# A weighted sum of gathered rows: kept in PSUM, with one pair of rows added ahead of the transposes

## The chip, the cores and the metric

One Trainium2 chip (trn2), one of its cores. The metric is the device time of one run in microseconds (us). The engines are called PE (TensorE; PEld is its weight load), DVE (VectorE), ACT (ScalarE), POOL (GpSimd, which also issues the indirect gathers) and SP (SyncE).

## The reference

Two graph layers over 3327 nodes with 512 features; the adjacency matrix `adj` is sparse (about 0.24% of it is set) and has a full diagonal. After each layer the input is added and the row is normalised. Layer 0 is a graph attention with 4 heads. Layer 1, which the change concerns, is cut here to its core:

```python
type_sum = adj @ x                                   # plain sum of the neighbours' rows
attn_a = sigmoid(concat([type_sum, x]) @ Wa.T + ba)  # one gate per node; attn_b likewise
h = x @ W_sa
scores = (h @ a_left)[:, None] + (h @ a_right)[None, :]
e = where(adj != 0, exp(-leaky_relu(scores, 0.01)), 0)
x_a = (e / (sum(e, axis=1) + 1e-5)) @ h              # weighted sum of the neighbours
x_b = adj @ (x @ W_gcnb) + b_gcnb                    # plain sum, projected
x = layernorm(x + sigmoid(attn_a * x_a + attn_b * x_b))
```

Since the projections are linear, a node needs two sums over its neighbours' rows of `x`: a weighted one (projected with `W_sa`) and a plain one (projected with `W_gcnb`).

## The kernel before, in words

Nodes are padded to 3328 and sorted by degree within two groups, so that 26 tiles of 128 nodes have few neighbour slots each: `CAPS` lists 4 to 14 per tile, 226 in all. Layer 0 leaves a table of rows in HBM (`table1`: 512 features and 8 columns of scores). For a tile, POOL issues one indirect gather per slot (`indirect`, L615), which brings one neighbour row for each of the 128 nodes into a slot of a ring of 42 row buffers in SBUF (`ring`). The node's own row is in SBUF already (`row1`). Two tiles (`T0`) have a further row, the "stair", for the few nodes with more neighbours; that makes 228 gathers in layer 1.

The tiles go through a software pipeline written out by hand: a loop over `i` in which tile `j` is summed, the next tile `j1` gets its weights, `jp` (the previous one) is projected, and `jpp` (the one before that) is gated, added and normalised. Within each engine instructions run in the order in which the loop writes them. One turn of the loop, by engine:

- POOL: `gather` issues every gather whose slots belong to a tile that was freed (`free(jp)`), then, when all gathers are out, the results are scattered to `out` (L146).
- PE: `turn(jp)` transposes the weighted sum (L1107), `plain_sum(j)` builds the plain sum, already transposed, by transposing the tile's own row and every neighbour row into one PSUM tile where they accumulate (L1098, four 128x128 transposes a row), and `project(jp, 1)`, `project(jp, 0)` multiply both sums of the previous tile by their weights (L1118, 16 matmul instructions).
- DVE: `weighted(j, 0)` runs the first part of the weighted sum, one multiply-add per slot (L1085: `sw = row * e + sw`, 128x512 fp32, all operands in SBUF), then come the gating of `jpp` (L1147, L1148, with the projections in PSUM as second input), the scores and weights of `j1` (`weights_a`, L1032 to L1052), the rest of the sum (`weighted(j, 1)`), the addition for `jpp` (L1171), `weights_b(j1)` (L1059 to L1062) and the statistics of `jpp` (L692, L693 and, for every fourth tile or so, the chain L701 to L708).
- ACT: copies of the two transposed sums to SBUF (`to_sbuf`, L1112), tanh and exp, and `scaled_first(j1)` (L1070), which starts the next weighted sum with the own row times its weight.

Each L1085 needs the result of the one before it. The cut between the two parts of a tile's sum:

```python
cut = 2 + (CAPS[j] * 5 + 7) // 8
for s0, n, g, _ in got[j]:
    for i in range(n):
        s = s0 + i
        if (s < cut) == (part == 0):
            nc.vector.scalar_tensor_tensor(sw, g[:, i, 0:F], e[:, s : s + 1], sw, ALU.mult, ALU.add)
```

[...]

Of the kernel before, what the change touches and what calls it, by code (L numbers as in the profile page):

```python
# [8 lines left out]
F32 = mybir.dt.float32  # L9
AF = mybir.ActivationFunctionType  # L10
ALU = mybir.AluOpType
# [3 lines left out]
P = 128  # L15
# [10 lines left out]
CAPS = (14, 12, 11, 10, 9, 9, 8, 8, 7, 6, 6, 5) + (14, 13, 11, 10, 10, 9, 9, 8, 8, 7, 7, 6, 5, 4)  # L26
# [52 lines left out]
def sparse_pass(  # L79
# [39 lines left out]
    nc = tc.nc  # L119
    N, F = out.shape  # L120
    NP = x.shape[0]
    H, FO = a_self.shape
    KT = F // P
# [5 lines left out]
    T0 = (0, NG[0])  # L129
    B = len(STAIRS)  # L130
# [45 lines left out]
    def place(j):  # L176

        return (0, j) if j < NG[0] else (1, j - NG[0])
# [5 lines left out]
    def row1(j):  # L184
        g, i = place(j)
        return x1[g][:, i, :]

    def slots(j):

        return S + 1 if j in T0 else CAPS[j] + 1  # L190
# [419 lines left out]
    got, stair = {}, {}  # L610
# [44 lines left out]
    def gather():  # L655

        while waiting and waiting[0][0] - freed[0] <= RING:
            indirect(*waiting.pop(0)[1:])

    def free(j):  # L660

        freed[0] = ends_at[j]
# [285 lines left out]
    for i in range(NT + 3):  # L948
# [10 lines left out]
        if 0 < i <= NT:  # L959
            j = order0[i - 1]  # L960
# [7 lines left out]
            if done:  # L968
                k0, scale, shift = done
# [30 lines left out]
    m1 = ctx.enter_context(tc.tile_pool(name="m1", bufs=2))  # L1000
    ps1 = ctx.enter_context(tc.tile_pool(name="ps1", bufs=1, space=PSUM, side="right"))
# [12 lines left out]
        order += long[:1] + short[:1]  # L1014
        short, long = short[1:], long[1:]
    order += last
    ew, gates, sums, plain, proj, zs, stair_sum = {}, {}, {}, {}, {}, {}, {}

    def own_score(j):
        ew[j] = m1.tile([P, S + 1], F32, tag="e", name=f"e{j}", bufs=3)  # L1020
        nc.scalar.copy(ew[j][:, 0:1], row1(j)[:, F + 6 : F + 7])

    def weights_a(j):

        c = slots(j)
        e = ew[j]
        gate = gates[j] = m1.tile([P, 12], F32, tag="gate", name=f"gate{j}", bufs=5)
        if j in T0:
            small = ps1.tile([P, B * H], F32, tag="small", name=f"to_nodes1_{j}")
            cols = to_nodes(m1, small, f"l1_{j}", stair[j][:, F : F + 3])  # L1030
        for s0, n, g, _ in got[j]:
            nc.vector.tensor_scalar(e[:, s0 : s0 + n], g[:, :n, F], row1(j)[:, F + 3 : F + 4], None, ALU.add)  # L1032
        if j in T0:
            nc.vector.scalar_tensor_tensor(
                e[:, C0 + 1 :], cols[:, :, 0], row1(j)[:, F + 3 : F + 4], no_step, ALU.add, ALU.subtract
            )
        nc.vector.scalar_tensor_tensor(e[:, :c], e[:, :c], 0.01, e[:, :c], ALU.mult, ALU.max)

        nc.scalar.activation(e[:, :c], e[:, :c], AF.Exp, scale=-1.0, accum_out=gate[:, 2:3])
        for i, (s0, n, g, _) in enumerate(got[j]):  # L1040
            nc.vector.tensor_reduce(
                gate[:, 4 + 2 * i : 6 + 2 * i], g[:, :n, F + 1 : F + 3].rearrange("p s i -> p i s"), AX.X, ALU.add
            )
        parts = len(got[j])
        if j in T0:
            nc.vector.tensor_reduce(
                gate[:, 4 + 2 * parts : 6 + 2 * parts], cols[:, :, 1:3].rearrange("p b i -> p i b"), AX.X, ALU.add
            )
            parts += 1
        nc.vector.tensor_add(gate[:, 0:2], gate[:, 4:6], row1(j)[:, F + 4 : F + 6])  # L1050
        for i in range(1, parts):
            nc.vector.tensor_add(gate[:, 0:2], gate[:, 0:2], gate[:, 4 + 2 * i : 6 + 2 * i])  # L1052

        nc.scalar.activation(gate[:, 0:2], gate[:, 0:2], AF.Tanh, scale=0.5)

    def weights_b(j):

        c, e, gate = slots(j), ew[j], gates[j]
        nc.vector.tensor_scalar(gate[:, 2:3], gate[:, 2:3], 1e-5, None, ALU.add)  # L1059
        nc.vector.tensor_scalar(gate[:, 0:2], gate[:, 0:2], 0.5, 0.5, ALU.mult, ALU.add)  # L1060
        nc.vector.reciprocal(gate[:, 2:3], gate[:, 2:3])
        nc.vector.tensor_scalar(e[:, :c], e[:, :c], gate[:, 2:3], gate[:, 0:1], ALU.mult, ALU.mult)  # L1062
        if j in T0:
            small = ps1.tile([P, B * H], F32, tag="small", name=f"to_rows1_{j}")
            ws2[j] = to_rows(m1, small, f"l1_{j}", e[:, C0 + 1 :].rearrange("p (b o) -> p b o", o=1))

    def scaled_first(j):

        sw = sums[j] = m1.tile([P, F], F32, tag="sw", name=f"sw{j}")
        nc.scalar.activation(sw, row1(j)[:, 0:F], AF.Copy, scale=ew[j][:, 0:1])  # L1070
        if j in T0:
            scaled = m1.tile([P, F], F32, tag="scaled", name=f"scaled{j}", bufs=1)
            nc.scalar.activation(scaled, stair[j][:, 0:F], AF.Copy, scale=ws2[j])
            stair_sum[j] = ps1.tile([P, F], F32, tag="stair", name=f"stair_sum{j}")
            nc.tensor.matmul(stair_sum[j], to_node, scaled, start=True, stop=True)  # L1075

    def weighted(j, part):

        e, sw = ew[j], sums[j]
        cut = 2 + (CAPS[j] * 5 + 7) // 8  # L1080
        for s0, n, g, _ in got[j]:
            for i in range(n):
                s = s0 + i
                if (s < cut) == (part == 0):
                    nc.vector.scalar_tensor_tensor(sw, g[:, i, 0:F], e[:, s : s + 1], sw, ALU.mult, ALU.add)  # L1085
        if part == 1 and j in T0:
            nc.vector.tensor_add(sw, stair_sum[j], sw)

    def plain_sum(j):


        pl = plain[j] = ps.tile([P, KT, P], F32, tag="acc", name=f"acc1_{j}", bufs=2)
        rows = [row1(j)] + [g[:, i, :] for _, n, g, _ in got[j] for i in range(n)]
        rows += [stair[j]] if j in T0 else []
        for i, row in enumerate(rows):
            steps = j in T0 and i == len(rows) - 1
            for k in range(KT):
                nc.tensor.matmul(  # L1098
                    pl[:, k, :], row[:, k * P : (k + 1) * P], to_node if steps else ident,
                    start=(i + k == 0), stop=(i == len(rows) - 1 and k == KT - 1), is_transpose=not steps,  # L1100
                )

    def turn(j):
# [10 lines left out]
    def project(j, half):  # L1114
        sT, wt = zs[j, half], (wsa, wg)[half]
        po = proj[j, half] = ps1.tile([P, F], F32, tag=f"po{half}", name=f"po{half}_{j}", bufs=1 + half)
        for k in range(KT):
            nc.tensor.matmul(po, sT[:, k, :], wt[:, k, :], start=(k == 0), stop=(k == KT - 1))  # L1118
# [12 lines left out]
    for i in range(NT + 3):  # L1131
        j, j1, jp, jpp = at_(i), at_(i + 1), at_(i - 1), at_(i - 2)
        if i > 0 and jp is not None:
            free(jp)
        gather()
        if j1 is not None:
            own_score(j1)
        if jp is not None:
            to_sbuf(jp, 1)
            turn(jp)  # L1140
            to_sbuf(jp, 0)
        if j is not None:
            plain_sum(j)
            weighted(j, 0)
        if jpp is not None:
            za = zs[jpp] = m1.tile([P, F], F32, tag="za", name=f"za{jpp}", bufs=3)
            nc.vector.tensor_add(za, bias_g, proj[jpp, 1])  # L1147
            nc.vector.scalar_tensor_tensor(za, za, gates[jpp][:, 1:2], proj[jpp, 0], ALU.mult, ALU.add)  # L1148
            nc.scalar.activation(za, za, AF.Tanh, scale=0.5)  # L1149
        if jp is not None:  # L1150
            project(jp, 1)
            project(jp, 0)
        if j1 is not None:
            weights_a(j1)
        if j is not None:
            weighted(j, 1)
        if ready:
            k0, scale, shift = ready
            for k in range(k0, i - 2):
                z = row1(order[k])[:, 0:F]  # L1160
                nc.scalar.activation(
                    z, z, AF.Identity, scale=scale[:, k - k0 : k - k0 + 1], bias=shift[:, k - k0 : k - k0 + 1]
                )
                outs.append((own(order[k]), z))
            ready = None
        while outs and not waiting:
            scatter("out", out, *outs.pop(0), N - 1)
        if jpp is not None:
            za = zs[jpp]
            zs[jpp] = row1(jpp)[:, 0:F]  # L1170
            nc.vector.scalar_tensor_tensor(zs[jpp], za, 0.5, zs[jpp], ALU.mult, ALU.add)  # L1171
        if j1 is not None:
            weights_b(j1)
            scaled_first(j1)
        if jpp is not None:
            ready = norm.add(i - 2, zs[jpp])
# [452 lines left out]
```

## Time and profile before

| | |
|---|---|
| median of 3 runs | 899.11 us (894.95 to 904.59) |
| profiled execution: its time, its span | 897.77 us, 895.8 us |
| first gather of layer 1 starts | 530.9 us |
| last gather of layer 1 ends | 843.4 us |
| layer 1's multiply-adds (L1085) | 226, first at 542.4 us, last ends at 865.5 us |
| last transpose of a weighted sum (L1107) starts | 872.3 us |
| granted PE clock over the span | 0.908 |

The profile is one execution seen by the hardware profiler. A line of the groups gives the kernel's line, the engine, the operation, output<-inputs, shape and count, then busy time and mean duration, then the engine's idle time ahead of these instructions and what ended it. A line of the timeline gives start, duration, engine, line, operation and, in brackets, the idle time before and its releaser. In both, an engine that waits for nothing is not necessarily the bound: it may stand ready while the data of another are late.

### The profile page before, as it was taken

To read this page: it belongs to the slowest core of one execution; us is meant where nothing else is said; L and a number is where in the kernel's file an instruction comes from. 1 tells how busy PE (TensorE), PEld (TensorE's weight loads), DVE (VectorE), ACT (ScalarE), POOL (GpSimd) and SP (SyncE) were. 2 spreads that over 40 slices of the span, in tenths; PEclk is the share of its full clock that TensorE was granted. 3 is DMA by queue.
4 is the path that set the end of the run, shared out by engine and by line. 5 is a ranking of instruction groups with operands and counts; after the bars stand their busy time and mean duration, and the time that the engine had idled before them with its cause. 6 is when DMAs were issued, how large, how long until landed. Compare 5 with 4: busy or idle time off the path is not lost. (4 is left out here: it accounts for less than half of the span.)

```text
span 895.8 us, 11378 instructions
## 1 busy us (share of the span) xinstructions
PE 745.3 (83%) x3118; PEld 457.4 (51%) x3118; DVE 693.3 (77%) x2032; ACT 272.0 (30%) x794; POOL 595.2 (66%) x641
## 2 busy tenths in 40 slices
PE   4698997416799978799999957987997999999992
PEld 3477775103445534344444435654764666666551
DVE  4288787896678858769898845957996999998973
ACT  0122221002335525444646512212222222232231
POOL 6711133566577777777777747777777777777772
PEclk9799999556899989889999967999898999999997
DMA  8989999999777878789777637677767777777641
GB/s 330 369 340 403 366 377 345 380 387 399 267 225 227 276 234 263 231 278 329 219 234 228 222 115 203 188 199 201 187 184 196 192 196 195 203 193 199 195 187 74
DMA packets 73352, 224.74 MB, mean 251 GB/s; under 512 B 12736, under 2 KB 16784, under 8 KB 72384
## 3 DMA queue, kind: packets, MB, share of 16 engines
q0 software_dynamic: 46368, 153.69, 56.9%
q1 hardware_dynamic: 24256, 68.13, 19.9%
q10 hardware_dynamic: 2656, 2.10, 0.7%
q8 instruction: 27, 0.44, 0.2%
q14 instruction: 45, 0.37, 0.1%
HBM read 203.02 MB, written 31.51 MB: 262 GB/s over the span
## 5 line engine op out<-in xcount | busy, mean ns | idle before, releaser
L615 POOL DMA_INDIRECT ring<-table,srt x464 | 475.7, 1025 | 162.1 <-issue 56.2
L803 PE MATMUL acc<-ring,ident 128*128 128x512 f32 x504 | 239.4, 619 | 18.9 <-DVE ring L802 12.9
L1085 DVE SCALAR_TENSOR_TENSOR sw<-ring,e,sw 128x512 f32<-128x512 f32 x226 | 169.8, 751 | 10.7 <-ACT sw L1070 4.2
L803 PEld LDWEIGHTS acc<-ring,ident 128*128 128x128 f32 x504 | 94.4, 196 | 130.3 <-issue 74.3
L371 PE MATMUL pf<-w,xc 128*128 128x260 f32 x416 | 102.9, 410 | 13.1 <-DVE w L311 13.1
L1098 PE MATMUL acc<-ident,ring 128*128 128x128 f32 x904 | 108.6, 280 | 6.2 <-DMA ring<-table,srt 6.1
L797 DVE TENSOR_TENSOR ring<-ring,w 128x512 f32<-128x512 f32 x176 | 111.8, 693 | 0.5
L1098 PEld LDWEIGHTS acc<-ident,ring 128*128 128x128 f32 x904 | 103.6, 145 | 8.1 <-DMA ring<-table,srt 8.1
L1118 PE MATMUL po<-wsa,sT 128*128 128x512 f32 x208 | 95.4, 602 | 4.6 <-DVE za L1148 2.3
L371 PEld LDWEIGHTS pf<-w,xc 128*128 128x128 f32 x416 | 84.1, 205 | 29.3 <-DVE w L311 13.8
L1118 PE MATMUL po<-wg,sT 128*128 128x512 f32 x208 | 93.6, 593 | 0.0
L795 ACT ACTIVATE ring<-ring,w 128x128 f32<-128x128 f32 x304 | 91.5, 390 | 0.0
L383 POOL DMA_DIRECT2D table<-row x26 | 14.2, 549 | 85.2 <-ACT st L380 82.6
L1118 PEld LDWEIGHTS po<-wsa,sT 128*128 128x128 f32 x208 | 39.7, 193 | 56.6 <-issue 56.1
L1118 PEld LDWEIGHTS po<-wg,sT 128*128 128x128 f32 x208 | 37.5, 190 | 37.3 <-issue 37.3
L1149 ACT ACTIVATE za<-za 128x512 f32<-128x512 f32 x26 | 16.4, 630 | 127.7 <-DVE za L1148 127.7
L402 PE MATMUL pc<-at,pow 128*32 128x512 bf16 (+1 forms) x182 | 23.3, 413 | 35.3 <-DMA at<-in_adjB 25.4
L762 ACT ACTIVATE w<-w 128x40 f32<-128x40 f32 (+10 forms) x26 | 6.2, 237 | 127.5 <-DVE w L761 127.5
L375 ACT COPY row<-pf 128x512 f32<-128x512 f32 x26 | 15.2, 586 | 95.4 <-PE pf L371 49.7
L834 PEld LDWEIGHTS pcol<-v,xt 128*128 128x128 f32 x208 | 28.7, 201 | 14.5 <-issue 12.1
L828 ACT COPY xt<-x1t 128x512 f32<-128x512 f32 x26 | 15.2, 584 | 62.9 <-PE x1t L822 62.9
L402 PEld LDWEIGHTS <-pow 128*32 128x32 bf16 x182 | 7.3, 97 | 47.9 <-issue 44.8
(252 smaller groups left out, 918.4 us busy)
## 6 DMA issues: line engine op xcount, KB each, us to landing
at<-in_adjB SPq DMA_DIRECT2D x78, 512.0 KB, 11.5
ring<-table,srt POOLq DMA_INDIRECT x464, 3.9
table<-row POOLq DMA_DIRECT2D x26, 260.0 KB, 6.1
xc<-in_xB SPq DMA_DIRECT2D x6, 1024.0 KB, 8.4
own<-in_xo SPq DMA_DIRECT2D x1, 3640.0 KB, 46.5
own<-table SPq DMA_DIRECT2D x1, 3640.0 KB, 55.2
at<-in_adjL SPq DMA_DIRECT2D x13, 256.0 KB, 9.9
table<-in_xo SPq DMA_DIRECT2D x1, 3120.0 KB, 27.2
```

The source lines that it names most:

```text
L371: nc.tensor.matmul(pf[:, hh, :HC], xc[:, k, o : o + P], w0[:, k, hh, :], start=(k == 0), stop=(k == KT - 1))
L375: nc.scalar.copy(row[:, 0:F].rearrange("p (h o) -> p h o", h=2), pf[:, :, 0 : F // 2])
L402: nc.tensor.matmul(pc[32 * c : 32 * c + 32, : nt * P], pow2[:, s, :], loaded[i, m], start=(s == 0), stop=(m + 1 not in ms or s == 3),)
L615: return nc.gpsimd.indirect_dma_start(out=out_, out_offset=None, in_=table, in_offset=bass.IndirectOffsetOnAxis(ap=ap, axis=0)).ins
L795: nc.scalar.activation(gv[:, h, :], gv[:, h, :], AF.Copy, scale=w[:, s, h : h + 1])
L797: nc.vector.tensor_tensor(gv, gv, w[:, s, :].rearrange("p (h o) -> p h o", o=1).to_broadcast([P, H, FO]), ALU.mult)
L803: nc.tensor.matmul(acc, ident, row, start=(lean and s == 0), stop=(s == CAPS[j] and j not in T0))
L834: nc.tensor.matmul(pcol, xt1[:, k, :], v1[:, k, :], start=(k == 0), stop=(k == KT - 1))
L1085: nc.vector.scalar_tensor_tensor(sw, g[:, i, 0:F], e[:, s : s + 1], sw, ALU.mult, ALU.add)
L1098: nc.tensor.matmul(pl[:, k, :], row[:, k * P : (k + 1) * P], to_node if steps else ident, start=(i + k == 0), stop=(i == len(rows) - 1 and ...
L1118: nc.tensor.matmul(po, sT[:, k, :], wt[:, k, :], start=(k == 0), stop=(k == KT - 1))
L1149: nc.scalar.activation(za, za, AF.Tanh, scale=0.5)
```

## The change

The running sum `so_far` moves to a PSUM tile: ACT writes the first product there, and every multiply-add reads its second input from it and writes its result to it, but for the last one of the tile, which writes the SBUF tile `sw` that PE transposes. The first two neighbour rows that lie side by side in the ring (`paired`) are also added by DVE, into the second one's slot, right after the multiply-add that uses that second row. PE leaves both rows out of `plain_sum(j, False)` and transposes their sum instead, in `plain_sum(j, True)`, after the projections of the previous tile. To make room in PSUM, the stair's sum shares the bank of `small`. The cut keeps the last multiply-add in the second part, also in tiles with 4 and 5 slots. Other engines' work and the order of the gathers stay as they are.

```diff
     def scaled_first(j):
 
-        sw = sums[j] = m1.tile([P, F], F32, tag="sw", name=f"sw{j}")
-        nc.scalar.activation(sw, row1(j)[:, 0:F], AF.Copy, scale=ew[j][:, 0:1])
+        so_far[j] = ps1.tile([P, F], F32, tag="so_far", name=f"so_far{j}")
+        nc.scalar.activation(so_far[j], row1(j)[:, 0:F], AF.Copy, scale=ew[j][:, 0:1])
...
-            stair_sum[j] = ps1.tile([P, F], F32, tag="stair", name=f"stair_sum{j}")
+            stair_sum[j] = ps1.tile([P, F], F32, tag="small", name=f"stair_sum{j}")
...
     def weighted(j, part):
 
-        e, sw = ew[j], sums[j]
-        cut = 2 + (CAPS[j] * 5 + 7) // 8
+        e, sw, two = ew[j], so_far[j], paired(j)
+        if part == 1:
+            sums[j] = m1.tile([P, F], F32, tag="sw", name=f"sw{j}")
+        cut = min(2 + (CAPS[j] * 5 + 7) // 8, CAPS[j])
...
-                    nc.vector.scalar_tensor_tensor(sw, g[:, i, 0:F], e[:, s : s + 1], sw, ALU.mult, ALU.add)
+                    to = sums[j] if s == CAPS[j] else sw
+                    nc.vector.scalar_tensor_tensor(to, g[:, i, 0:F], e[:, s : s + 1], sw, ALU.mult, ALU.add)
+                    if two is not None and s == two + 1:
+                        nc.vector.tensor_add(g[:, i, 0:F], g[:, i - 1, 0:F], g[:, i, 0:F])
...
+    def paired(j):
+
+        for s0, n, g, _ in got[j]:
+            if n > 1:
+                return s0
+        return None
+
+    def plain_sum(j, sum_of_two):
...
+        rows = [(s0 + i, g[:, i, :]) for s0, n, g, _ in got[j] for i in range(n)]
+        if sum_of_two:
+            rows = [row for s, row in rows if s - 1 == two]
+        else:
+            rows = [row1(j)] + [row for s, row in rows if two is None or s not in (two, two + 1)]
+            rows += [stair[j]] if j in T0 else []
...
         if j is not None:
-            plain_sum(j)
+            plain_sum(j, False)
             weighted(j, 0)
...
             project(jp, 1)
             project(jp, 0)
+        if j is not None:
+            plain_sum(j, True)
```

More of the change, by code (lines that the diff above doesn't have):

```diff
@@ L1016, in sparse_pass @@
     order += last
-    ew, gates, sums, plain, proj, zs, stair_sum = {}, {}, {}, {}, {}, {}, {}
+    ew, gates, sums, plain, proj, zs, stair_sum, so_far = {}, {}, {}, {}, {}, {}, {}, {}
     def own_score(j):
@@ L1028, in weights_a @@
         if j in T0:
-            small = ps1.tile([P, B * H], F32, tag="small", name=f"to_nodes1_{j}")
+            small = ps1.tile([P, F], F32, tag="small", name=f"to_nodes1_{j}")
             cols = to_nodes(m1, small, f"l1_{j}", stair[j][:, F : F + 3])
@@ L1063, in weights_b @@
         if j in T0:
-            small = ps1.tile([P, B * H], F32, tag="small", name=f"to_rows1_{j}")
+            small = ps1.tile([P, F], F32, tag="small", name=f"to_rows1_{j}")
             ws2[j] = to_rows(m1, small, f"l1_{j}", e[:, C0 + 1 :].rearrange("p (b o) -> p b o", o=1))
     def scaled_first(j):
-        sw = sums[j] = m1.tile([P, F], F32, tag="sw", name=f"sw{j}")
-        nc.scalar.activation(sw, row1(j)[:, 0:F], AF.Copy, scale=ew[j][:, 0:1])
+        so_far[j] = ps1.tile([P, F], F32, tag="so_far", name=f"so_far{j}")
+        nc.scalar.activation(so_far[j], row1(j)[:, 0:F], AF.Copy, scale=ew[j][:, 0:1])
         if j in T0:
@@ L1084, in weighted @@
                 if (s < cut) == (part == 0):
-                    nc.vector.scalar_tensor_tensor(sw, g[:, i, 0:F], e[:, s : s + 1], sw, ALU.mult, ALU.add)
+                    to = sums[j] if s == CAPS[j] else sw
+                    nc.vector.scalar_tensor_tensor(to, g[:, i, 0:F], e[:, s : s + 1], sw, ALU.mult, ALU.add)
+                    if two is not None and s == two + 1:
+                        nc.vector.tensor_add(g[:, i, 0:F], g[:, i - 1, 0:F], g[:, i, 0:F])
         if part == 1 and j in T0:
[L1087 to L1094, printed above, removed]
+            nc.vector.tensor_add(sums[j], stair_sum[j], sums[j])
+    def paired(j):
[4 more added lines that the diff above has]
+    def plain_sum(j, sum_of_two):
+        two = paired(j)
+        if not sum_of_two:
+            plain[j] = ps.tile([P, KT, P], F32, tag="acc", name=f"acc1_{j}", bufs=2)
+        elif two is None:
+            return
+        pl = plain[j]
+        rows = [(s0 + i, g[:, i, :]) for s0, n, g, _ in got[j] for i in range(n)]
[4 more added lines that the diff above has]
+            rows += [stair[j]] if j in T0 else []
         for i, row in enumerate(rows):
-            steps = j in T0 and i == len(rows) - 1
+            steps = j in T0 and not sum_of_two and i == len(rows) - 1
+            last_one = (sum_of_two or two is None) and i == len(rows) - 1
             for k in range(KT):
@@ L1099, in plain_sum @@
                     pl[:, k, :], row[:, k * P : (k + 1) * P], to_node if steps else ident,
-                    start=(i + k == 0), stop=(i == len(rows) - 1 and k == KT - 1), is_transpose=not steps,
+                    start=(i + k == 0 and not sum_of_two), stop=(last_one and k == KT - 1), is_transpose=not steps,
                 )
```

## The prediction

> **What bounds the kernel now.** I read the page first, then busy time by stretches, then VectorE's waits, then the timeline of one steady stretch. The change touches layer 1 only, which runs from 530.9 us (first gather of layer 1) to the end of the span at 895.8 us.
>
> ```profile
> PE 745.3 (83%) x3118; PEld 457.4 (51%) x3118; DVE 693.3 (77%) x2032; ACT 272.0 (30%) x794; POOL 595.2 (66%) x641
> L615 POOL DMA_INDIRECT ring<-table,srt x464 | 475.7, 1025 | 162.1 <-issue 56.2
> L1085 DVE SCALAR_TENSOR_TENSOR sw<-ring,e,sw 128x512 f32<-128x512 f32 x226 | 169.8, 751 | 10.7 <-ACT sw L1070 4.2
> L1098 PE MATMUL acc<-ident,ring 128*128 128x128 f32 x904 | 108.6, 280 | 6.2 <-DMA ring<-table,srt 6.1
> ```
>
> The page's shares average two layers and prove nothing for this one. The stretches do (columns: sum, then busy us of PE, PEld, DVE, ACT, POOL, then PE clock, DMA share, GB/s):
>
> ```profile
> 690.00:806.00 116.00, 116.00 (x624) 80.59 (x623) 108.44 (x240) 31.16 (x81) 90.15 (x85) 0.99 0.72 195
> 540.00:896.00 356.00, 314.13 (x1536) 207.28 (x1535) 291.46 (x694) 92.69 (x235) 264.64 (x247) 0.94 0.66 186
> ```
>
> Three engines are full at once in 690 to 806. PE is busy all 116 us. DVE's 108.4 plus the 35 ns that pass between dependent instructions fill the stretch. POOL's 90.15 plus a constant 0.30 us before each of 85 gathers is 115.6. So which one sets the end is read from who waits for data:
>
> ```profile
> DVE e L1032 <- DMA ring<-table,srt: 25.9, 6, 11.6
> DVE spread_l L668 <- DMA ring<-table,ids: 8.6, 2, 5.9
> ```
>
> VectorE waits for gathered rows 8 times. Less the first 11.6 us, that is 22.9 us; the timeline puts 8.88 us of it at 592.9 (the sixth tile in the order, 13 rows), 2.70 at 622, 5.88 at 682, 0.84 at 810, and the rest in the first three tiles. POOL never waits for a ring slot: its gathers run without a break from 530.9 to 843.4 us, 228 in 312.5 us, 1.37 us each. So POOL sets the pace up to 682, VectorE from there to about 850, and PE the last tiles (idle for 2.3 us in all between 700 and 880).
>
> POOL's pace has a cause that the timeline shows:
>
> ```profile
> 704.14 4.72 DVE L1085 SCALAR_TENSOR_TENSOR sw<-ring,e,sw 128x512 f32<-128x512 f32 x6
> 704.20 0.95 POOL L615 DMA_INDIRECT ring<-table,srt  x1 [0.30 <-DVE mvn L693]
> 705.45 1.08 POOL L615 DMA_INDIRECT ring<-table,srt  x1 [0.30 <-DMA ring<-table,srt]
> 706.83 1.27 POOL L615 DMA_INDIRECT ring<-table,srt  x1 [0.30 <-PE po L1118]
> 709.55 0.75 DVE L1148 SCALAR_TENSOR_TENSOR za<-za,gate,po 128x512 f32<-128x512 f32 x1
> 709.97 0.95 POOL L615 DMA_INDIRECT ring<-table,srt  x1 [0.30 <-PE acc L1098]
> 712.49 0.68 DVE L1171 SCALAR_TENSOR_TENSOR x1a<-za,x1a 128x512 f32<-128x512 f32 x1
> 713.09 0.14 DVE L1059 TENSOR_SCALAR gate<-gate 128x1 f32<-128x1 f32 x1
> ```
>
> A gather takes 0.945 us, or longer if an L1085 is under way about 0.125 us after its start: it then ends later by what was left of that L1085. The six L1085 stand 0.79 us apart ((4.72 - 0.75)/5), one from 706.53 to 707.28; the gather of 706.83 loses 707.28 - 706.955 = 0.325 us and takes 1.27. L1148, whose second tensor is in PSUM, spans the gather of 709.97 and costs it nothing. Set against VectorE in this way, 115 of the 228 gathers met an L1085 and 94 were stretched, by 27.1 us in all; everything else stretched them by 0.8 us.
>
> [...] (27.1 us beside L1085; 23 gathers beside L1147, L1148 and L1087, which have one input in PSUM, lost nothing). [...]
>
> ```profile
> L1148 DVE SCALAR_TENSOR_TENSOR za<-za,gate,po 128x512 f32<-128x512 f32 x26 | 19.4, 747 | 5.9 <-PE po L1118 3.5
> L1147 DVE TENSOR_TENSOR za<-bias_g,po 128x512 f32<-128x512 f32 x26 | 17.6, 679 | 0.0
> L1087 DVE TENSOR_TENSOR sw<-stair_sum,sw 128x512 f32<-128x512 f32 x2 | 1.4, 692 | 0.2
> ```
>
> L1148 with a PSUM input takes 747 ns, L1085 without 751; L1147 and L1087 with one take 679 and 692, the page's L797 without (layer 0, the same size) 693. No run here shows VectorE writing to PSUM.
>
> **The change part by part.**
>
> 1. *Multiply-adds read and write PSUM* (226 instructions). The second input leaves SBUF, so the 27.1 us of stretched gathers should go; gathers then come every 0.945 + 0.30 = 1.25 us. The step itself, 0.787 us start to start because each needs the one before, is unknown with a PSUM output. Below: the reads save 1 to 14 ns in the rows above, and I allow a write that saves 55 ns more. [...] I take 10 ns less. The last multiply-add of a tile writes SBUF for the transposes. PSUM has one running sum instead of two in SBUF, yet ScalarE's first product of the next tile already comes after L1062, which VectorE runs after the last multiply-add: no new wait. Nor is there one from sharing a PSUM buffer between the small step matrices and the stair sum, which follow each other anyway.
>
> 2. *The pair add* (26, one per tile), 128x512 SBUF inputs. The built order has it between two multiply-adds, waiting for VectorE's own semaphore (it overwrites a row the multiply-add before it reads); the multiply-add behind it carries no such wait. So it starts 0.787 us after that one, as a dependent one does, and the next starts 0.60 us later, as L1059 starts after L1171 (713.09 - 712.49). One step of 0.787 becomes 0.787 + 0.607: 0.607 us per tile, 15.8 us over 26. Bounds: 0.49 if it need not wait, 0.79 if both waits count. It still blocks gathers; L1171, as often and as long, stretched them by 0.7 us in total.
>
> 3. *PE loses one row per tile*: 4 transposes at 0.109 us (a row of four every 0.437 us in the timeline), 0.437 us, 11.4 us over 26. The pair's sum is transposed after the projections, so the row and its ring slot are held some 7 us longer. That delays no gather on the path: a slot filled at 806 us was last used by a tile that VectorE had finished at 774, and gathers some 20 us faster keep over 10 us of that. PE's wait for the add is hidden, since the add runs early in the tile's chain and the next PE item, the turn (L1107), needs the chain's end.
>
> 4. *Smaller:* in tiles with 4 or 5 rows the last multiply-add moves behind the previous tile's gating; the last such tile had 6.8 us to spare (chain ends 865.5, turn 872.3).
>
> *The sum.* VectorE's arrival at the sixth tile is set by data: 43 gathers, the 43rd ending 588.8 now, 4.1 us before VectorE starts at 592.9. At 1.25 us it ends 530.9 + 43 x 1.25 - 0.3 = 584.4, so VectorE starts at 588.5 (on its own it arrives at 584.0 + 5 x 0.607 = 587.0 at the latest). From 592.9 to the end of the 24th tile's chain at 849.4 are 256.5 us, of which 2.70 + 5.88 + 0.84 = 9.4 are data waits; the faster gathers end these. Afterwards: 588.5 + 247.1 + 19 adds x 0.607 (11.5) - 187 rows x 0.010 (1.9) = 845.2, 4.2 earlier. PE's turn of that tile, now 3.5 us behind the chain because PE is full, follows at once: 845.3 against 852.9, 7.6 earlier. From there PE does two short tiles, 19.4 us now, less two rows: 18.5. The last turn is at 863.9 against 872.3, and VectorE's last chain ends at 862.4, in time. What follows, 23.5 us to the end, stays. The end moves by 8.4 us: 897.77 - 8.4 = 889.4 us. The profiled execution lies 1.3 us under the median of 899.11 and inside the runs' 894.95 to 904.59; I leave the figure as it is. What is late next is VectorE: PE alone needs 157 us from the twelfth turn to the last (165.7 now, less 2.3 idle and 14 rows of 0.437); from the twelfth chain's new end, 692, it would be there by 850.
>
> **The rivals.**
>
> *PSUM shortens the chain* (a step of 0.745 us or less). For: reads of PSUM come out shorter in every pair of rows above. Against: nothing shows the write. Each 10 ns is worth 1.9 us until PE bounds at about 850 for the last turn; 40 to 70 ns give 876 to 884 us.
>
> *PSUM lengthens the chain*; the slower end. [...] an in-place sum reads and writes the same buffer in each instruction. Against: L1148's 747 ns. [...] It decides from about 90 ns on (a step of 0.88 us): 889.4 + 187 x 0.10 = 908.1, 1% over the median, and 1.9 us more per 10 ns.
>
> *The gathers are not relieved*, the change doing no more than moving work from PE to VectorE. For: the block is inferred from times. Against: the 23 gathers beside PSUM inputs. The data waits at 622 and 682 then swallow the adds before them, and 13 adds after 682 cost 7.9, less 0.84 of wait and 1.2 of PSUM; with PE's slack of 3.5 and two rows saved, +1.5: 899.3 us.
>
> **How the numbers follow.** Forecast as summed, step within 30 ns of today's: 0.50, 884 to 894 us. Shorter chain: 0.20. Longer chain by 30 to 90 ns: 0.13; by more: 0.10, with all else that could make it slower 0.02 more. Not relieved: 0.05. About 1% is what a measurement of this kernel can tell from no change. Below 890.1 (1% under the median) lie three fifths of the forecast's 0.50 and the shorter chain: 0.50 faster. Same: the rest of the forecast, the moderate lengthening and the unrelieved case, 0.38. Slower 0.12. The range, 876 to 903, runs from a step 70 ns shorter [...].
>
> **What would show it.** Right: gathers of layer 1 at 0.95 us beside the multiply-adds, almost all; 26 adds at about 0.69 us and 0.61 us to the next start; data waits after 592 gone; PE with gaps before the turns; the last turn about 864. Wrong: gathers still at 1.27, or a multiply-add step far from 0.78 us; the step times 187 then says how far the end moves.

## The result and the profile after

The changed kernel takes 906.06 us (median of 20 runs, 900.98 to 910.02); the kernel before takes 897.09 us in the runs beside it (893.06 to 904.59). The ratio of the runs is 1.0085, interval 1.0068 to 1.0102: slower by 0.85% (the two medians alone differ by 1.0%), where 889.4 us was predicted. The profiled execution of the changed kernel took 907.42 us, its span 905.4 us.

The page of the changed kernel (engine totals, then groups: line, engine, operation, count, busy us, mean ns, idle before and its releaser):

```profile
PE 740.4 (82%) x3014; PEld 446.5 (49%) x3014; DVE 708.1 (78%) x2058; ACT 272.1 (30%) x794; POOL 570.4 (63%) x641
L615 POOL DMA_INDIRECT ring<-table,srt x464 | 454.4, 979 | 168.3 <-issue 62.1
L1088 DVE SCALAR_TENSOR_TENSOR so_far<-ring,e,so_far 128x512 f32<-128x512 f32 x200 | 150.7, 754 | 8.6 <-ACT so_far L1070 4.0
L1139 PE MATMUL po<-wsa,sT 128*128 128x512 f32 x208 | 101.9, 636 | 19.1 <-DVE e L1032 10.3
```

Every part of the change shows. POOL is 24.8 us less busy (570.4 against 595.2): the gathers' mean fell from 1025 to 979 ns over both layers. VectorE has 26 more instructions and 14.8 us more work. PE has 104 transposes fewer, which were to save 11.4 us, yet it is only 4.9 us less busy: its projections through `wsa` (L1139, L1118 before) went from 95.4 to 101.9 us, 636 ns each instead of 602, and they now stand behind 19.1 us of idle time instead of 4.6.

The groups of layer 1 give the pair add and ACT's first product, now written to PSUM (687 ns, 719 before):

```profile
L1090 DVE TENSOR_TENSOR ring<-ring 128x512 f32<-128x512 f32 x26 | 18.0, 692 | 0.9
L1070 ACT ACTIVATE so_far<-x1b,e 128x512 f32<-128x512 f32 x14 | 9.6, 687 | 28.5 <-DVE e L1062 28.5
```

The stretch from 690 to 806 us in the same columns as before (sum, PE, PEld, DVE, ACT, POOL, PE clock, DMA share, GB/s):

```profile
690.00:806.00 116.00, 106.73 (x532) 71.23 (x533) 108.76 (x240) 31.57 (x79) 82.49 (x86) 0.96 0.71 196
```

PE and POOL are no longer full there (116.00 and 90.15 before); VectorE still is. The turning point is in VectorE's waits (who waited, for whom, total us, times, longest):

```profile
DVE e L1032 <- DMA ring<-table,srt: 18.8, 4, 11.7
DVE e L1034 <- PE to_nodes L673: 12.6, 2, 6.9
```

Before, VectorE waited 34.5 us for gathered rows and 0.4 us for `to_nodes`, the two small matmuls with which PE spreads the stair's scores over the nodes of a `T0` tile. Now it waits 18.8 us for rows, 11.7 of them at the first tile, and 12.6 us for `to_nodes`, all of it at the two stair tiles. There lay nearly all of the 9.4 us that faster gathers were to win.

The timeline of PE at the first stair tile, changed kernel (start, duration, operation, count, idle before and releaser):

```profile
610.81 3.60 PE L1139 MATMUL po<-wg,sT 128*128 128x512 f32 x8
618.12 6.48 PE L1139 MATMUL po<-wsa,sT 128*128 128x512 f32 x8 [3.71 <-DVE spread_l L668]
624.43 0.60 PE L1119 MATMUL acc<-ident,ring 128*128 128x128 f32 x4
624.87 0.30 PE L673 MATMUL to_nodes<-spread_l,to_node 128*128 128x30 f32 x2
```

And of VectorE in the same stretch:

```profile
617.23 0.75 DVE L1169 SCALAR_TENSOR_TENSOR za<-za,gate,po 128x512 f32<-128x512 f32 x1
617.89 0.18 DVE L668 TENSOR_TENSOR spread_l<-step_of,ring 128x30 f32<-128x30 f32 x1
...
625.21 0.23 DVE L1034 SCALAR_TENSOR_TENSOR e<-to_nodes,x1b,no_step 128x10 f32<-128x10 f32 x1 [6.86 <-PE to_nodes L673]
```

The data are there: L668 runs at 617.89, 4.1 us earlier than before (621.95). But `to_nodes` is in PE's queue behind `project(jp, 0)`. That projection writes `po0`, which has a single buffer (`po1` has two), still held by the projection of two tiles earlier until L1169 has read it at 617.98. So PE stands idle for 3.71 us. (The profile names L668, which ends a moment later; L1169 is what holds the buffer.) Then the eight matmuls take 6.48 us, where the eight above them took 3.60, and only after them and the pair's transposes does `to_nodes` run. The clock granted to PE over these eight was 0.56 (the last three numbers are clock, DMA share and GB/s); over the eight above it was 1.00:

```profile
618.12:624.60 6.48, 6.48 (x10) 2.80 (x11) 0.23 (x2) 0.52 (x1) 4.73 (x5) 0.56 0.75 214
```

The same stretch of the kernel before:

```profile
619.40 3.67 PE L1118 MATMUL po<-wsa,sT 128*128 128x512 f32 x8 [2.29 <-DVE za L1148]
622.91 0.30 PE L673 MATMUL to_nodes<-spread_l,to_node 128*128 128x30 f32 x2
...
621.95 0.19 DVE L668 TENSOR_TENSOR spread_l<-step_of,ring 128x30 f32<-128x30 f32 x1 [2.70 <-DMA ring<-table,ids]
...
623.25 0.23 DVE L1034 SCALAR_TENSOR_TENSOR e<-to_nodes,x1b,no_step 128x10 f32<-128x10 f32 x1 [0.42 <-PE to_nodes L673]
```

The projection was held up by the same buffer then (2.29 us), and was done at 623.07. It lay under the wait for data: the 0.42 us in the last line is all that stuck out. `to_nodes` followed the projection at once, so earlier data could have won nothing at this tile. At the second stair tile, also before:

```profile
677.68 3.60 PE L1118 MATMUL po<-wsa,sT 128*128 128x512 f32 x8
682.18 0.41 PE L673 MATMUL to_nodes<-spread_l,to_node 128*128 128x30 f32 x2 [0.91 <-DVE spread_l L668]
```

PE was free 0.91 us before the scores came. So of the 2.70 and 5.88 us of data waits at these two tiles, 0.9 us was to be had if PE's work ahead of `to_nodes` ended no earlier.

### The profile page after: what moved, and what is told of

Read it like the earlier page. It is cut to its first block, busy times and chain, and to the rows that moved or that the text cites. A ratio compares the mean times of both kernels' runs of the same rounds, so it can differ in the third digit from the quotient of the medians.

```text
span 905.4 us, 11178 instructions
## 1 busy us (share of the span) xinstructions
PE 740.4 (82%) x3014; PEld 446.5 (49%) x3014; DVE 708.1 (78%) x2058; ACT 272.1 (30%) x794; POOL 570.4 (63%) x641
## 5 line engine op out<-in xcount | busy, mean ns | idle before, releaser
L615 POOL DMA_INDIRECT ring<-table,srt x464 | 454.4, 979 | 168.3 <-issue 62.1
L803 PE MATMUL acc<-ring,ident 128*128 128x512 f32 x504 | 239.8, 620 | 17.7 <-DVE ring L802 11.7
L1088 DVE SCALAR_TENSOR_TENSOR so_far<-ring,e,so_far 128x512 f32<-128x512 f32 x200 | 150.7, 754 | 8.6 <-ACT so_far L1070 4.0
L1139 PE MATMUL po<-wsa,sT 128*128 128x512 f32 x208 | 101.9, 636 | 19.1 <-DVE e L1032 10.3
L1119 PE MATMUL acc<-ident,ring 128*128 128x128 f32 x800 | 101.1, 281 | 12.2 <-DMA ring<-table,srt 8.2
L1119 PEld LDWEIGHTS acc<-ident,ring 128*128 128x128 f32 x800 | 93.8, 146 | 27.1 <-issue 12.8
L371 PEld LDWEIGHTS pf<-w,xc 128*128 128x128 f32 x416 | 84.1, 205 | 29.4 <-DVE w L311 13.8
L1139 PE MATMUL po<-wg,sT 128*128 128x512 f32 x208 | 93.8, 594 | 0.3 <-ACT sT L1133 0.3
L1139 PEld LDWEIGHTS po<-wsa,sT 128*128 128x128 f32 x208 | 41.4, 204 | 77.1 <-issue 76.5
L1170 ACT ACTIVATE za<-za 128x512 f32<-128x512 f32 x26 | 16.4, 630 | 150.9 <-DVE za L1169 150.9
L1139 PEld LDWEIGHTS po<-wg,sT 128*128 128x128 f32 x208 | 37.7, 192 | 37.8 <-issue 37.3
L402 PE MATMUL pc<-at,pow 128*32 128x512 bf16 (+1 forms) x182 | 23.5, 420 | 36.4 <-DMA at<-in_adjB 26.7
```

Of the source, the lines that this page charges most:

```text
L371: nc.tensor.matmul(pf[:, hh, :HC], xc[:, k, o : o + P], w0[:, k, hh, :], start=(k == 0), stop=(k == KT - 1))
L402: nc.tensor.matmul(pc[32 * c : 32 * c + 32, : nt * P], pow2[:, s, :], loaded[i, m], start=(s == 0), stop=(m + 1 not in ms or s == 3),)
L615: return nc.gpsimd.indirect_dma_start(out=out_, out_offset=None, in_=table, in_offset=bass.IndirectOffsetOnAxis(ap=ap, axis=0)).ins
L803: nc.tensor.matmul(acc, ident, row, start=(lean and s == 0), stop=(s == CAPS[j] and j not in T0))
L1088: nc.vector.scalar_tensor_tensor(to, g[:, i, 0:F], e[:, s : s + 1], sw, ALU.mult, ALU.add)
L1119: nc.tensor.matmul(pl[:, k, :], row[:, k * P : (k + 1) * P], to_node if steps else ident, start=(i + k == 0 and not sum_of_two), stop=(las ...
```

## The experiments

Each was compared with the kernel before on the same chip (896.7 to 897.6 us). Since the start of layer 1 varies by a few us between executions, two points of each profiled execution (one for each kernel) are also given, counted from the first gather of layer 1: the start of the tile behind the second stair tile (its first L1032, under another line number where the edit moves it), and the start of the last transpose of a weighted sum. The prediction's 157.2 is its arrival at the sixth tile, 57.6, and the 104.7 us that follow in the kernel before, less 8.6 of data waits, with seven pair adds and 72 rows at its prices.

| | median us | ratio to before (interval) | tile behind the stair | last transpose |
|---|---|---|---|---|
| before | 897.09 | | 166.6 | 341.4 |
| prediction for the change | 889.4 | | 157.2 | 333.0 |
| changed | 906.06 | 1.0085 (1.0068 to 1.0102) | 170.8 | 349.7 |
| changed, `to_nodes` early | 897.37 | 1.0009 (0.9992 to 1.0026) | 162.3 | 341.9 |
| changed, gating first | 893.29 | 0.9963 (0.9946 to 0.998) | 158.4 | 335.0 |
| sum in PSUM, no pair | 889.84 | 0.9914 (0.9888 to 0.994) | 161.9 | 334.3 |
| the same, `to_nodes` early | 882.48 | 0.9847 (0.9813 to 0.988) | 154.8 | 327.6 |
| the same, gating first | 887.47 | 0.9882 (0.9849 to 0.9916) | 160.3 | 331.6 |
| pair alone, sum in SBUF | 905.89 | 1.0095 (1.0063 to 1.0127) | 171.9 | 351.1 |
| before, `to_nodes` early | 897.55 | 1.0 (0.9986 to 1.0014) | 166.8 | 341.4 |

**`to_nodes` early.** The changed kernel with the stair's small matmuls ahead of `project(jp, 0)` in PE's queue. `stair_scores(j1)` holds the two lines of `to_nodes`, which are taken out of `weights_a` (not shown):

```diff
             project(jp, 1)
+            if j1 in T0:
+                stair_scores(j1)
             project(jp, 0)
```

> The same kernel as stair_early, on another occasion, since there the kernel before itself took 1077 us: the changed kernel with the to_nodes matmul of the two stair tiles ahead of project(jp, 0) on TensorE's queue. My theory: VectorE's wait at L1034 falls from 12.6 us to under 2 us and the time to 893 to 897 us, if the kernel before is at its 897. Rival (VectorE's added work is the loss): the wait goes, the time stays within 3 us of 906.

It took 897.37 us, 8.7 less than the changed kernel and 0.4 more than the upper end of the theory. VectorE's waits:

```profile
DVE own_step_l L682 <- PE to_rows L680: 5.8, 2, 3.9
DVE e L1039 <- PE to_nodes L673: 0.7, 2, 0.5
```

The wait for `to_nodes` is gone (12.6 to 0.7 us). Part of it comes back one step later: `to_rows`, which carries the stair's weights, now stands behind the slow projection (6.61 us at the first stair tile), and VectorE waits 5.8 us for it (1.3 in the changed kernel). The net 7.4 us are most of the 8.5 us by which the tile behind the stair begins earlier, and of the 8.7 us in the time. PE still waits for `po0` to be read.

**Gating first.** The changed kernel, with VectorE's gating of `jpp`, which frees `po0`, ahead of the first part of the weighted sum. `to_nodes` keeps its place:

```diff
             plain_sum(j, False)
-            weighted(j, 0)
         if jpp is not None:
             za = zs[jpp] = m1.tile([P, F], F32, tag="za", name=f"za{jpp}", bufs=3)
             nc.vector.tensor_add(za, bias_g, proj[jpp, 1])
...
+        if j is not None:
+            weighted(j, 0)
```

The half speed that the next text names is the granted clock of 0.50 that the changed kernel shows from 619 to 621 us, behind 3.71 us of idle time.

> The changed kernel, with one change of order on VectorE: the two gating instructions that read the projections of two tiles before come ahead of the first part of the weighted sum, not behind it. They free the only buffer of the second projection some 5 us earlier, so that TensorE never stands idle for it. The stair score matmuls stay behind that projection. Theory (that buffer, and the half speed of TensorE after the idle time, hold the stair matmuls up): VectorE's wait for them falls from 12.6 us to under 4 us, no projection takes more than 9 us, and the time is 895 to 901 us. Rival (the place in the queue alone decides): the wait stays over 8 us and the time over 903 us. VectorE may meet a new wait for the projection at the start of a short tile; over 2 us each at several tiles would show that.

893.29 us: 12.8 less than the changed kernel, and more than expected. Its timeline at the first stair tile:

```profile
606.06 3.60 PE L1139 MATMUL po<-wg,sT 128*128 128x512 f32 x8
609.50 3.60 PE L1139 MATMUL po<-wsa,sT 128*128 128x512 f32 x8
...
614.34 0.41 PE L673 MATMUL to_nodes<-spread_l,to_node 128*128 128x30 f32 x2 [0.81 <-DVE spread_l L668]
```

No gap ahead of the second projection, no slow matmuls, and `to_nodes` now waits for VectorE. None of the 26 tiles has a pair of projections longer than 7.1 us but the first (7.4); in the changed kernel the longest was 13.8. VectorE's waits:

```profile
DVE za L1168 <- PE po L1139: 7.2, 7, 2.7
...
DVE e L1034 <- PE to_nodes L673: 1.0, 2, 0.8
```

The new wait that was feared, for projections at the start of a tile, is there, but costs 7.2 us in all (2.3 in the changed kernel), less than the 11.6 us that went. This separates the two parts of the cause: in the changed kernel the queue order matters only because the buffer holds up what stands ahead of `to_nodes`.

**The kernel before, `to_nodes` early.** The control: the same move as above in the kernel before.

> The kernel before, with nothing changed but the small stair score matmuls, which move ahead of the second projection in TensorE's queue. Theory: here VectorE waits for gathered rows at both stair tiles and for TensorE only 0.4 us, so the move brings nothing: within 2 us of the kernel before. Rival (the move is good in any kernel): 4 us or more faster.

897.55 us, ratio 1.0, and both points of the table within 0.2 us of the kernel before. There VectorE still waits for the data of both stair tiles (2.67 and 3.27 us ahead of L668). It also waits longer for `to_rows`, 4.4 us where it was 1.5, and the second tile's data wait is shorter by about as much (5.88 before). The move is no gain of its own; it is worth 7 to 9 us (889.84 to 882.48 below, 906.06 to 897.37 above) only once the data are no longer late.

**The sum in PSUM, no pair.** `paired` returns nothing, so all rows are transposed and VectorE adds none:

```diff
     def paired(j):
-        for s0, n, g, _ in got[j]:
-            if n > 1:
-                return s0
         return None
```

> The running sum in PSUM and the shared small bank as in the changed kernel, but no pair add: TensorE transposes every neighbour row again, and the small stair matmuls stay behind the two projections. Theory (the pair add costs VectorE 0.61 us a tile, and the stair tiles' wait for TensorE's queue comes on top of it): without the adds VectorE arrives 15 us earlier at the last tiles, TensorE becomes the bound, and the stair wait is still there at the two stair tiles, so 884 to 892 us, that is 2 to 10 us above the same kernel with the early stair matmuls (882.5). Rival (the PSUM sum itself is what costs, the adds are hidden): 900 us or more.

889.84 us, as the first theory had it, with the stair wait present:

```profile
DVE e L1034 <- PE to_nodes L673: 8.5, 2, 5.2
```

**The same, `to_nodes` early.**

> The same kernel as no_pair_stair_early on another occasion: the sum in PSUM, no pair, to_nodes ahead of project(jp, 0). My theory: 878 to 886 us beside 897 of the kernel before. Rival (TensorE bounds at its old pace): 890 to 896 us.

882.48 us, 1.5% faster than the kernel before and the fastest of all here. `to_nodes` costs VectorE 1.5 us and `to_rows` 1.1. PE stands idle for `po0` for 2.7 us in all (15.9 with the pair), since it has 104 more transposes and comes to the projection later.

The pair's price follows: 906.06 - 889.84 = 16.2 us with `to_nodes` late, 897.37 - 882.48 = 14.9 us with it early. The prediction had 26 x 0.607 = 15.8 us of VectorE time, but these differences aren't that term alone: the pair also brings PE's idle time and the slow projections behind it. With gating first, where both are absent, it costs 893.29 - 887.47 = 5.8 us (next experiment); there the kernel without the pair is held up by PE.

**The same, gating first.** No pair, sum in PSUM, gating ahead of the weighted sum, `to_nodes` late.

> The same kernel as in the run before (no pair add, the running sum in PSUM, the gating ahead of the first part of the weighted sum), now against a kernel before that takes 897 us and not 1080. If the early gating and the early stair matmuls remove one and the same stall: 879 to 886 us, with VectorE's wait for the stair matmuls under 4 us. If the early gating also gains elsewhere: below 879 us. If TensorE then makes VectorE wait for the projections at the start of many tiles: 887 us or more.

887.47 us: neither of the first two guesses, but the third. Here PE transposes all rows again and comes late with the projections, and VectorE, which now wants them at the start of each tile, waits:

```profile
DVE za L1165 <- PE po L1136: 14.9, 9, 2.7
DVE e L1034 <- PE to_nodes L673: 3.1, 2, 2.6
```

So gating first is good with the pair, where PE has time. Without it the median is 5.0 us above that of the early `to_nodes`, a difference which the runs hardly separate: the intervals of the two ratios overlap (0.9849 to 0.9916, 0.9813 to 0.988).

**The pair alone.** The kernel before with the pair add and PE's missing row, but with the running sum, its first product included, in SBUF. Set against the changed kernel, `so_far` and `sums` become one SBUF tile, so that every multiply-add reads and writes it:

```diff
-        so_far[j] = ps1.tile([P, F], F32, tag="so_far", name=f"so_far{j}")
+        so_far[j] = sums[j] = m1.tile([P, F], F32, tag="sw", name=f"sw{j}")
...
-        if part == 1:
-            sums[j] = m1.tile([P, F], F32, tag="sw", name=f"sw{j}")
```

> The pair add and the missing row on TensorE as in the changed kernel, the running sum in SBUF as in the kernel before. Theory: gathers beside the multiply-adds are stretched again (mean near 1.05 us), so the two stair tiles are reached with their data late, which swallows part of the adds; later adds cost 0.61 us each and nothing gives them back: 899 to 907 us. Rival (the PSUM sum is what makes the changed kernel slow): 890 to 896 us.

905.89 us, the changed kernel's time. Its page and VectorE's waits:

```profile
L615 POOL DMA_INDIRECT ring<-table,srt x464 | 476.2, 1026 | 162.1 <-issue 59.3
DVE e L1032 <- DMA ring<-table,srt: 21.9, 4, 11.5
DVE e L1034 <- PE to_nodes L673: 8.5, 2, 5.5
DVE spread_l L668 <- DMA ring<-table,ids: 2.3, 1, 2.3
```

The gathers are as slow as in the kernel before, and the stair tiles still wait for PE; data are late by 2.3 us at the first of them and not at the second. So beside the pair, the sum in PSUM brings nothing that the times show (906.06 against 905.89; ratios 1.0085 and 1.0095), although it relieves the gathers beside the multiply-adds: the pair has already made VectorE late enough for most of the data, and where it arrives early it meets `to_nodes` (12.6 us against 8.5). Without the pair the same move brings 7.3 us (897.19, the kernel before in that comparison, less 889.84), and with `to_nodes` early 14.2 (896.69, again the kernel before beside it, less 882.48).

**On slower chips.** Five of the kernels also ran on two chips where the kernel before itself took 1076.7 and 1079.8 us, at a granted clock near 0.84 where the table's runs have about 0.90. None of the five is shown to be faster than the kernel before there, the table's fastest included, so what the table shows doesn't stand for such chips. In the trace of the one without the pair and with gating first VectorE waits 54.5 us for `acc` in layer 1, in three waits, where the same kernel at 887.47 us has no such wait; why is open. The edits are those shown above.

> The changed kernel without its pair add: VectorE adds no pair, TensorE transposes every row, the running sum stays in PSUM. My theory (the change lost at the two stair tiles, where VectorE waits for TensorE's to_nodes matmul, 12.6 us in all, and paid 0.61 us a tile for the pair): the 19 to 26 adds go (11 to 16 us of VectorE), the waits at the stair tiles stay at 9 to 14 us, the time falls to 893 to 898 us, about that of the kernel before. Rival 1 (TensorE was the bound and the pair pays for itself): slower than 906, by up to 11 us. Rival 2 (the sum in PSUM is the loss, whatever the trace says of its step): stays at 903 or more.

1082.63 us, ratio 1.0113 (1.0004 to 1.0223).

> The pair add alone: the running sum goes back to SBUF, the rest is the changed kernel. My theory: gathers beside the multiply-adds are stretched to 1.27 us again (about 27 us over layer 1), VectorE waits for data at the stair tiles as in the kernel before, and these waits swallow part of the adds; 898 to 902 us. Rival 1 (the adds are the whole loss of the change): 905 to 908 us. Rival 2 (the PSUM sum is the whole loss): at or below the kernel before, 890 to 897 us.

1088.04 us, without a ratio.

> The changed kernel with one move: for the two stair tiles the to_nodes matmul stands on TensorE's queue ahead of project(jp, 0) and not behind it and the pair's transposes. My theory: VectorE's wait at L1034 falls from 12.6 us to under 2 us, everything behind it comes earlier, and the time falls by 9 to 13 us to 893 to 897 us. Rival (VectorE's added work is the loss, the wait is only where slack shows up): the wait goes but the time stays within 3 us of 906.

1080.07 us, ratio 1.0005 (0.9961 to 1.0048).

> The sum in PSUM, no pair, and the to_nodes matmul ahead of project(jp, 0). My theory: both losses go and the faster gathers are left: VectorE's last chain ends about 25 us before the changed kernel's 878 us, TensorE becomes the bound, 878 to 886 us, clearly under the kernel before. Rival (with the pair gone TensorE bounds at its old pace): 890 to 896 us.

1078.77 us, ratio 1.0047 (1.0002 to 1.0091).

> No pair add, the running sum in PSUM, the gating ahead of the first part of the weighted sum, the small stair score matmuls at their old place behind the second projection. If the early gating and the early stair matmuls remove one and the same stall, this gives what the kernel without pair and with the early stair matmuls gave, 882.5 us: 879 to 886 us, with VectorE's wait for the stair matmuls under 4 us. If the early gating also gains elsewhere (no wait of TensorE for the projection's buffer at any tile), it is below 879 us. If TensorE, which transposes all rows again, then makes VectorE wait for the projections at the start of many tiles, it is 887 us or more.

1085.3 us, ratio 1.0129 (1.001 to 1.0249).

## Why the prediction was wrong, step by step

*The block between gathers and multiply-adds: right.* Set against VectorE as in the prediction, 107 gathers met an L1088 and lost 0.2 us in all (27.1 before); in the kernel with the pair alone 109 met the multiply-add and lost 24.2 us. Pair adds and L1194 stretched 24 gathers of the changed kernel by 5.8 us, where L1171 had cost 0.7: a miss that cost little, since behind the sixth tile no gather was late any more.

*The multiply-add's step: mis-sized.* From starts in the trace it is 791 ns (787 before), not 777: the write to PSUM saves nothing and costs next to nothing. Over 187 rows the 14 ns are 2.6 us. No trace of the kernel before showed VectorE writing to PSUM; the 10 ns less, and the lengthening behind the range's 903 us, were assumptions.

*The pair add: right on VectorE.* From L1088 to L1090 791 ns, from L1090 to the next L1088 610 ns; 0.61 us per tile against 0.607. In the times the pair cost 16.2, 14.9 and 5.8 us in three orders of the queues; that the first two lie near 15.8 is in part chance, as they hold PE's losses too. The held row and slot cost nothing on the path, as was said: POOL once waits for a slot (7.8 us, up to 711.5), and no wait of VectorE for data follows.

*The arrival at the sixth tile: 1.6 us late.* VectorE starts at 590.1 and not at 588.5. The 43rd gather ends at 586.5 where 584.4 was predicted: 0.9 us is the first gather's start, 531.8 against 530.9, and 1.1 us went to four gathers stretched by pair adds and L1194. VectorE then starts 3.6 us behind it, not 4.1.

*The 9.4 us of data waits: the step that failed.* "The faster gathers end these" holds for the waits as the profile names them: no row is late at the stair tiles. The time did not come back. Behind the two data waits there, 8.58 us together, stood `to_nodes`, 0.4 us later at the first tile, and it took their place with 12.6 us. The prediction names no wait of VectorE at these tiles but that for data; it did not ask when PE would be done if the data came sooner. The 0.42 us ahead of L1034 in the kernel before was no sign of slack, it was what stuck out of a longer wait. And the change made that second wait longer itself: without the pair VectorE waits 8.5 us there instead of 12.6, and PE stands idle 1.50 us ahead of the first stair tile's projection instead of 3.71. The likely reason is that with the pair PE reaches `project(jp, 0)` earlier, by its missing row, and VectorE frees `po0` later, by the pair add before the gating.

*What PE saves: a second term that failed.* The prediction let PE win 0.437 us per tile and lose nothing. Of the 11.4 us of transposes, 6.5 went back into slower projections (95.4 to 101.9 us): PE idles for `po0`, and after the longer gaps the matmuls run slow. The changed kernel's timeline at three gaps:

```profile
742.97 3.67 PE L1139 MATMUL po<-wsa,sT 128*128 128x512 f32 x8 [1.88 <-DVE e L1032]
794.59 5.29 PE L1139 MATMUL po<-wsa,sT 128*128 128x512 f32 x8 [2.78 <-DVE e L1032]
846.17 5.09 PE L1139 MATMUL po<-wsa,sT 128*128 128x512 f32 x8 [2.99 <-DVE e L1032]
```

After 1.88 us of idle time they keep their speed in this kernel, after 2.78 and more they do not. The last of them is on the path: it delays the turns of the 23rd and 24th tiles, and the latter starts 2.7 us behind its chain (860.1, 862.8), where the prediction had it follow at once. Its reading of the kernel before was wrong here: that turn was 3.5 us behind not simply because PE was full, but because PE had stood idle at the same place and then run slowly (5.37 us instead of 3.60, granted clock 0.68), 3.7 us in all:

```profile
836.02 5.37 PE L1118 MATMUL po<-wsa,sT 128*128 128x512 f32 x8 [1.94 <-DVE e L1032]
```

*The sum.* The 24th chain ends at 860.1, 14.9 us behind the predicted 845.2: 12.2 of stair waits (12.6 less the 0.4 of before), 1.6 of the arrival, 2.6 of the step make 16.4; VectorE's waits for ACT's first product and for `to_rows` came out 0.8 us shorter, and 0.7 us less stays unassigned. With PE's 2.7 us the last transpose comes at 881.5, 17.6 behind 863.9. The rest to the end, 23.9 us, was put at 23.5. With gating first, which removes both failed terms and keeps the change, the last transpose comes 335.0 us after the first gather against the 333.0 of the sum. The step's 2.6 us are about that size; the rest hasn't been traced term by term.

*The rivals.* None of them was this one. The longer chain and the unrelieved gathers are excluded by their own numbers, a step of 791 ns and 0.2 us lost, and a time beyond the range was reached by a mechanism that was not on the list: a wait of one engine on another, hidden beneath the data wait. The kernel with the pair alone is close to the case that the unrelieved rival summed to 899.3 us (its step was put 10 ns shorter); it took 905.89. That sum has the same gap, since it lets the data waits at the stair tiles swallow the adds and leaves out the 8.5 us for `to_nodes`.

## What to carry to other kernels

A data wait that is to be removed can have a second one beneath it: before its length is booked as a gain, follow every other input of the waiting instruction back through its own queue, and ask when it would have been ready. Work taken from an engine can be worth little if that engine's next instruction needs a buffer that a busier engine frees; look for the oldest reader of each single buffer and try that reader further forward. An exchange of PE work for VectorE work (here 11.4 us for 15.8) paid in none of the three orders tried, and it has to be tried apart from the parts it comes with: here the PSUM sum alone gained and the pair lost.

## What the runs showed of the hardware

PE's matmuls ran slow after some short gaps. In the changed kernel eight matmuls took 5.1 to 6.5 us instead of 3.6 to 3.7 after four gaps of 2.78 to 3.71 us, at a granted clock of 0.56 to 0.72 (0.50 from 619 to 621 us); after six gaps of 0.6 to 1.9 us they kept their speed, at 1.00. The gap's length alone does not decide it: in the changed kernel with `to_nodes` early a gap of 3.43 us cost nothing (3.67 us), and in the kernel before one of 1.94 us did (5.37 us, clock 0.68). What lowers the granted clock was not shown.

An accumulation in PSUM instead of SBUF left VectorE's multiply-add as long as it was (754 against 751 ns). Beside it the gathers of layer 1 lost 0.2 us in all, where they had lost 27.1. ACT's product was shorter when it went to PSUM (687 against 719 ns).
